# A graph network on one core: the sums start from each node's own row, and the last tiles' steps are placed anew

## The chip, the core and the metric

The kernel runs on one core of a Trainium2 chip. A core has several engines that work side by side, each with its own stream of instructions, done in order: PE multiplies matrices and transposes through a multiplication with the identity matrix; DVE does elementwise work; ACT does functions of one variable and also issues transfers; POOL (GpSimd) here does little else than gather rows of a table in memory by an index; SP issues plain transfers. An engine waits for another by semaphores. SBUF is the memory on the core, of 128 partitions; PSUM is the small memory, in banks, that PE writes its results to.

The metric is the time of one execution on the device, in microseconds (us). The kernel before takes 4307.19 us, the median of 3 runs (4305.39 to 4313.39).

## What is computed

A network over a graph of 12,500 nodes with 256 features each, and 200,000 edges sorted by their target `dst`. Cut to what matters:

```python
def gcn_conv(x, W, b, src, dst, n):          # src, dst hold the edges and one loop per node
    h = x @ W
    deg = segment_sum(ones, dst, n)
    dinv = where(deg > 0, rsqrt(deg), 0)
    return segment_sum(h[src] * (dinv[src] * dinv[dst])[:, None], dst, n) + b

h = maximum(layernorm(x), 0)
h = h @ W_pre + b_pre
h = relu(gcn_conv(h, W1, b1, src + loops, dst + loops, n))
h = relu(gcn_conv(h, W2, b2, src + loops, dst + loops, n))
x = x + h @ W_post + b_post

h = maximum(layernorm(x), 0)
xt = (h @ weight).reshape(n, 4, 64)
alpha = softmax(leaky_relu(alpha_l(xt)[src] + alpha_r(xt)[dst]), over the heads)
x = x + broadcast(sum over the heads of alpha[:n] * xt[dst[:n]])
```

Each convolution adds up, for every node, the rows of the sources of its edges and the node's own row (the loop). The last layer uses only the first n edges, one for each output row.

## The kernel before

**Tiles and chunks.** Nodes are taken 128 at a time: 98 node tiles (`NT`). Edges are taken 128 at a time too, one gather for each such group; 14 gathers (`J`) make a chunk. There are 112 chunks (`NCH`), the last one of 9 gathers, so 1563 gathers in a convolution.

**Stages.** `fast_path` first computes the degrees and the normed rows, scaled by `dinv`, and writes them to `table1` in memory. Convolution one reads `table1` and writes `table2`; convolution two reads `table2`, adds the residual and writes `table_l` and `table_r` (what the attention layer needs of each row) and `kept_x`. The attention stage gathers from those and writes the output. A table must be written in full before the first gather of the next stage reads it. For the attention stage POOL first gathers seven blocks from `table_r` (which only covers the first tiles), then, after PE and ACT have made `fxg` of the first group, gathers `fal` from `table_l` (L1199).

**The loop of a convolution** (`convolve`). The order of instructions is that of the code (`manual_schedule`). For every gather POOL brings 128 rows into one of 64 buffers `fgot` (L999). DVE has made, once per chunk, a matrix `fhot` of ones and zeros (L939) that says to which target within the chunk's window of 128 nodes each edge goes. PE multiplies the two into the PSUM bank `facc` (L1004); 14 such multiplications add up a chunk.

At the end of a chunk `close` lays out three things. ACT copies `facc` to SBUF as `fsums` (L946). Later PE transposes it into the bank `fturn` (`turn`, L952 and L954). Later still DVE adds that to a sliding buffer of sums `buf` (`add`, L962; in convolution one also a row of extra sums, L965), at a column that it reads from a register, since a chunk's window lies anywhere among the `BW` = 448 columns that the buffer covers. After an addition that completes a node tile, `shift` makes a new buffer: it zeroes the last 128 columns (L974) and copies the others down (L975; L977 and L978 for the extra row). Then the finished tile goes through the steps of `finish1` or `finish2`.

**Due times.** `close` and `shift` don't issue these steps at once. They put them into a list with a due time, counted in gathers: `at(t + 8, turn)` means after the multiplication of the eighth gather from here. `run(t)`, called after every gather's multiplication, issues what is due. The steps of a tile that need the same single PSUM bank as another tile's are held apart by `fills` and `taken`: a step that fills a bank first runs the step that reads what the bank holds.

`finish1` (offsets in gathers): 0 `a` loads the tile's own rows `self` and the row `fins` on SP; 6 `b` transposes them into the bank `fpt` (`turned`, L1014, and L1029); 8 `c` adds them to the sums into `fin` (L1033, L1034); 14 `d` multiplies by the weights into `fpo` (L1039, and L1040 for the bias); 16 `e` applies relu on ACT (L1044) and writes 128 rows of `table2` (L1045, a transfer that ACT issues).

`finish2`: 0 `a` loads own rows, `rm` and the rows `fxb` of x; 6 `b` (L1014) and 8 `c` (L1074) as above; 14 `d` first weights into `fpz` (L1080, L1082); 16 `e` relu (`fz`, L1087); 20 `f` second weights into `fpo` (L1092, L1093); 22 `g` adds the residual (`fx`, L1097), stores it to `kept_x` and takes its statistics; 24 `h` norms (L1108 to L1113); 28 `i` transposes into `fpt` (L1014); 30 `k` copies that to `ht` (L1120); 34 `q` multiplies into `fpx` (L1128); 36 `r` copies it (L1133) and writes `table_l` and, for the first tiles, `table_r` (L1134, L1136).

**The end of a convolution.** Chunk 109 completes tile 94, chunk 110 tile 95, and the last chunk the tiles 96 and 97. From chunk 109 on (`near`) the offsets are halved, and the second of the two last tiles is shifted two gathers after the first:

```python
near = c + 3 >= NCH
then = None
for o, step, fills in reversed(finish(state["w"], buf, sbuf)):
    then = at(now + (o // 2 if near else o), lambda _, step=step: step(), fills, then)
...
if state["w"] < complete[c + 1]:
    at(now + (2 if near else J), shift)
```

After the last gather `run()` issues all that is left in order of due time.

Of the kernel before, what the change touches and what calls it, by code (L numbers as in the profile page):

```python
# [17 lines left out]
P = 128  # L18
# [395 lines left out]
def fast_path(  # L414
# [58 lines left out]
    XW = (M * (AC - 1) + OFF + P - 1) // P + 1  # L473
    assert AC * J == NT and AC * CE <= E and XW <= NT
    table_r = dram.tile([XW * P, DR], F32, name="table_r")
# [412 lines left out]

    def convolve(ep, table, stride, width, ahead, with_sum, psum, finish):

# [3 lines left out]
        state = {"w": 0, "n": 0}  # L894
        due, taken = [], {}

        def at(t, step, fills=None, then=None):
# [23 lines left out]
        def new_buf():  # L921
            buf = work.tile([P, KC, BW], F32, name="buf", bufs=5)
            sbuf = work.tile([1, BW], F32, name="sbuf", bufs=5) if with_sum else None
            return buf, sbuf

        state["buf"] = new_buf()
        for b in state["buf"]:
            if b is not None:
                nc.vector.memset(b, 0.0)

# [12 lines left out]
        def close(c, acc, t):  # L943

            sb = work.tile([P, width], F32, name="fsums", bufs=3)
            nc.scalar.activation(sb, acc, AF.Copy)  # L946
            v = {}

            def turn(_):
                v["pt"] = psum.tile([P, KC + 1, P], F32, name="fturn", bufs=1)  # L950
                for k in range(KC):
                    nc.tensor.transpose(v["pt"][:, k, :], sb[:, k * P:(k + 1) * P], ident)  # L952
                if with_sum:
                    nc.tensor.transpose(v["pt"][:1, KC, :], sb[:, D:D + 1], ident)  # L954

            def add(now):
                buf, sbuf = state["buf"]
                off = nc.values_load(offs[0:1, c:c + 1], engines=(mybir.EngineType.DVE,),
                                     min_val=0, max_val=OFF,
                                     skip_runtime_bounds_check_because="clamped on the chip")  # L960
                b = buf[:, :, bass.ds(off, P)]
                nc.vector.tensor_add(b, b, v["pt"][:, :KC, :])  # L962
                if with_sum:
                    b = sbuf[:, bass.ds(off, P)]
                    nc.vector.tensor_add(b, b, v["pt"][:1, KC, :])  # L965
                shift(now)

            def shift(now):
                if state["w"] == complete[c + 1]:
                    return  # L970

                buf, sbuf = state["buf"]
                nxt, nxs = new_buf()
                nc.vector.memset(nxt[:, :, BW - P:], 0.0)  # L974
                nc.vector.tensor_copy(nxt[:, :, :BW - P], buf[:, :, P:])  # L975
                if with_sum:
                    nc.vector.memset(nxs[:, BW - P:], 0.0)  # L977
                    nc.vector.tensor_copy(nxs[:, :BW - P], sbuf[:, P:])  # L978

                near = c + 3 >= NCH  # L980
                then = None
                for o, step, fills in reversed(finish(state["w"], buf, sbuf)):
                    then = at(now + (o // 2 if near else o), lambda _, step=step: step(),
                              fills, then)
                state["w"] += 1
                state["buf"] = nxt, nxs
                if state["w"] < complete[c + 1]:
                    at(now + (2 if near else J), shift)

            at(t + 8, turn)  # L990
            at(t + 13, add)

# [17 lines left out]

    def turned(psum, s):
        pt = psum.tile([P, KC + 1, P], F32, name="fpt", bufs=1)
        for k in range(KC):
            nc.tensor.transpose(pt[:, k, :], s[:, k * P:(k + 1) * P], ident)  # L1014
        return pt


    def finish1(psum, w, buf, sbuf):
        v = {}

        def a():
            v["s"] = work.tile([P, D1], F32, name="self", bufs=4)
            nc.sync.dma_start(v["s"], table1[w * P:(w + 1) * P, :])
            v["fs"] = work.tile([2, P], F32, name="fins", bufs=4)
            nc.sync.dma_start(v["fs"][1:2, :], root_t[w:w + 1, :])

        def b():
            v["pt"] = turned(psum, v["s"])
            nc.tensor.transpose(v["pt"][:1, KC, :], v["s"][:, D:D + 1], ident)  # L1029

        def c():
            v["f"] = work.tile([P, KC, P], F32, name="fin", bufs=3)
            nc.vector.tensor_add(v["f"], buf[:, :, :P], v["pt"][:, :KC, :])  # L1033
            nc.vector.tensor_add(v["fs"][:1, :], sbuf[:, :P], v["pt"][:1, KC, :])  # L1034

        def d():
            po = v["po"] = psum.tile([P, D], F32, name="fpo", bufs=1)
            for k in range(KC):
                nc.tensor.matmul(po, v["f"][:, k, :], wf[:, k, :], start=(k == 0), stop=False)  # L1039
            nc.tensor.matmul(po, v["fs"], bb, start=False, stop=True)  # L1040

        def e():
            o = work.tile([P, D], F32, name="fo", bufs=3)
            nc.scalar.activation(o, v["po"], AF.Relu, scale=dinv2[:, w:w + 1])  # L1044
            nc.scalar.dma_start(table2[w * P:(w + 1) * P, :], o)  # L1045

        return [(0, a, None), (6, b, "fpt"), (8, c, None), (14, d, "fpo"), (16, e, None)]

    with tc.tile_pool(name="psum1", bufs=1, space=PSUM) as psum, \
            tc.tile_pool(name="edges1", bufs=1) as ep, \  # L1050
            tc.tile_pool(name="fwork1", bufs=2) as work:
        convolve(ep, table1, D1, D + 1, 64, True, psum, lambda w, b, s: finish1(psum, w, b, s))


    def finish2(psum, w, buf, sbuf):
        v = {}
        n = min(P, N - w * P)

        def a():
            v["s"] = work.tile([P, D], F32, name="self2", bufs=4)  # L1060
            nc.sync.dma_start(v["s"], table2[w * P:(w + 1) * P, :])
            v["rm"] = work.tile([1, P], F32, name="rm", bufs=4)
            nc.sync.dma_start(v["rm"], root_t[w:w + 1, :])
            v["x"] = work.tile([P, D], F32, name="fxb", bufs=4)
            if n < P:
                nc.vector.memset(v["x"], 0.0)
            nc.sync.dma_start(v["x"][:n, :], x[w * P:w * P + n, :])

        def b():
            v["pt"] = turned(psum, v["s"])  # L1070

        def c():
            v["f"] = work.tile([P, KC, P], F32, name="fin", bufs=3)
            nc.vector.tensor_add(v["f"], buf[:, :, :P], v["pt"][:, :KC, :])  # L1074

        def d():
            pz = v["pz"] = psum.tile([P, KC, P], F32, name="fpz", bufs=1)
            for m in range(KC):
                for k in range(KC):
                    nc.tensor.matmul(pz[:, m, :], wb[:, k, m * P:(m + 1) * P], v["f"][:, k, :],  # L1080
                                     start=(k == 0), stop=False)
                nc.tensor.matmul(pz[:, m, :], b2r[:, m * P:(m + 1) * P], v["rm"],  # L1082
                                 start=False, stop=True)
# [5 lines left out]
        def f():  # L1089
            po = v["po"] = psum.tile([P, D], F32, name="fpo", bufs=1)  # L1090
            for m in range(KC):
# [23 lines left out]
        def i():  # L1115
            v["pt2"] = turned(psum, v["h"])

# [7 lines left out]
        def q():  # L1125
            px = v["px"] = psum.tile([P, DA], F32, name="fpx", bufs=1)
            for k in range(KC):
                nc.tensor.matmul(px[:, d0:], v["ht"][:, k, :], wg[:, k, d0:],  # L1128
                                 start=(k == 0), stop=(k == KC - 1))

        def r():
            xa = work.tile([P, DA], F32, name="fxa")
            nc.scalar.activation(xa[:, d0:], v["px"][:, d0:], AF.Copy)  # L1133
            nc.scalar.dma_start(table_l[w * P:(w + 1) * P, :], xa[:, DR:])  # L1134
            if w < XW:
                nc.scalar.dma_start(table_r[w * P:(w + 1) * P, :], xa[:, :DR])  # L1136

        return [(0, a, None), (6, b, "fpt"), (8, c, None), (14, d, "fpz"), (16, e, None),
                (20, f, "fpo"), (22, g, None), (24, h, None), (28, i, "fpt"), (30, k, None),
                (34, q, "fpx"), (36, r, None)]  # L1140


# [15 lines left out]
    with tc.tile_pool(name="psum2", bufs=1, space=PSUM) as psum, \  # L1158
            tc.tile_pool(name="edges2", bufs=1) as ep, \
            tc.tile_pool(name="fwork2", bufs=2) as work:  # L1160
        for c in range(EARLY):
            turn_hots(ap, c, load_ends(work, c, 1), EARLY)
        convolve(ep, table2, D, D, 64, False, psum, lambda w, b, s: finish2(psum, w, b, s))

# [123 lines left out]
```

## Time and profile before

| what | us |
|---|---|
| median of 3 runs | 4307.19 |
| the profiled execution by its own clock | 4960.23 |
| its span, first to last instruction | 4958.2 |
| PE busy | 2964.7 (60%) |
| weight loads of PE (beside PE) | 2202.3 (44%) |
| POOL busy | 3115.8 (63%) |
| DVE busy | 1148.5 (23%) |
| ACT busy | 383.4 (8%) |
| gathers of both convolutions, L999, 3126 of them | 2984.3 busy, 955 ns each |

The profile is of one execution, taken with the hardware profiler; it took 653 us longer than the median of the runs. A line of the timeline gives the start, the duration (both us), the engine, the line of the kernel, the operation, what it writes and reads, and in brackets how long the engine had stood idle and what released it. The table of stretches gives for each stretch its length, the busy time of each engine with the number of its instructions, then the clock that PE was granted (1 is full speed), the share of time in which transfers ran, and the GB/s. Where it is asked for one engine alone, there is one busy column. In the table of waits a line gives an engine, what waited and what released it, and then the total wait in us, the number of waits and the longest.

### The profile page before, as it was taken

The numbers are of one execution on the slowest core, as the hardware profiler recorded it, in microseconds if no ns is written. First come the engines' busy times: TensorE is split into PE (matmuls) and PEld (weight loads), VectorE is DVE, ScalarE is ACT, GpSimd is POOL, SyncE is SP. The second block draws the span as 40 slices with busy tenths as digits, with TensorE's granted clock in tenths as the row PEclk, the third lists the DMA queues.
The fourth block names the chain that finished last, engine by engine and source line by source line (L and its number), as shares of the span: only waits on it lengthen the run. The fifth ranks groups of instructions, "written<-read, shape, count | busy, mean of one in ns | idle before, by whom it ended". The sixth has DMA issues, their size and how long they took to land.

```text
span 4958.2 us, 34772 instructions
## 1 busy us (share of the span) xinstructions
PE 2964.7 (60%) x10827; PEld 2202.3 (44%) x10827; DVE 1148.5 (23%) x2468; ACT 383.4 (8%) x1054; POOL 3115.8 (63%) x3297
## 2 busy tenths in 40 slices
PE   5345555564555556465626767666777677677853
PEld 4133444343343334344414555555555555555642
DVE  7211111121111212112202222222222222222227
ACT  3100000000000000000000000000000000000112
POOL 2566666666666666666466666666666666666533
PEclk7567777677777777777757777777777777777766
DMA  5433333333333333333333443444444443444335
GB/s 179 133 93 105 106 106 105 104 108 104 106 105 105 104 105 106 105 106 104 101 93 112 113 112 105 113 108 107 110 109 109 110 108 108 109 110 108 97 97 157
DMA packets 301046, 543.62 MB, mean 110 GB/s; under 512 B 84021, under 2 KB 199476, under 8 KB 300852
## 3 DMA queue, kind: packets, MB, share of 16 engines
q0 software_dynamic: 154480, 414.28, 31.3%
q1 hardware_dynamic: 114926, 111.19, 7.4%
q10 hardware_dynamic: 31446, 15.83, 1.1%
q8 instruction: 88, 1.44, 0.1%
q14 instruction: 106, 0.87, 0.1%
HBM read 488.01 MB, written 52.93 MB: 109 GB/s over the span
## 4 chain that ended last, share of the span: by engine, by line
another core or an unknown queue 36%; PE 32%; issue 19%; DVE 4%; ACT 3%; POOL 1%; DMA 1%; ACTq 0%; DVEq 0%; POOLq 0%; SPq 0%
PE facc L1004 18%; PE fpo L1092 3%; PE fpo L1039 2%; PE fpx L1128 2%; PE fpo L1093 2%; PE fpo L1040 1%; POOL fgot L999 1%; PE fturn L952 1%; ACT h L1113 1%; PE fpt L1014 1%; PE fpz L1080 1%; DVE fhot L939 1%; DVE fx L1097 1%; PE fpz L1082 1%
## 5 line engine op out<-in xcount | busy, mean ns | idle before, releaser
L999 POOL DMA_INDIRECT fgot<-ftable,fsrc_t x3126 | 2984.3, 955 | 1595.4 <-issue 822.5
L1004 PE MATMUL facc<-fgot,fhot 128*128 128x257 f32 (+1 forms) x6252 | 1901.8, 456 | 218.1 <-issue 157.2
L1004 PEld LDWEIGHTS facc<-fgot,fhot 128*128 128x128 f32 x6252 | 1392.8, 233 | 564.6 <-issue 297.0
L952 PE MATMUL fturn<-fident,fsums 128*128 128x128 f32 x448 | 117.3, 355 | 626.9 <-issue 484.8
L939 DVE TENSOR_TENSOR fhot<-iota_p,to_t 128x1792 f32<-128x1792 f32 x224 | 447.6, 2000 | 0.1
L952 PEld LDWEIGHTS fturn<-fident,fsums 128*128 128x128 f32 x448 | 75.9, 184 | 690.4 <-issue 529.0
L946 ACT ACTIVATE fsums<-facc 128x257 f32<-128x257 f32 (+1 forms) x224 | 86.2, 385 | 3586.5 <-remote 2411.7
L1097 DVE SCALAR_TENSOR_TENSOR fx<-fpo,fdinv,fxb 128x256 f32<-128x256 f32 x98 | 47.4, 484 | 1289.1 <-PE fpo L1093 837.2
L1039 PE MATMUL fpo<-wf,fin 128*128 128x256 f32 x392 | 142.4, 499 | 329.1 <-issue 242.9
L1128 PE MATMUL fpx<-fwg,ht 128*128 128x4 f32 (+1 forms) x392 | 99.1, 363 | 391.3 <-ACT ht L1120 359.5
L1033 DVE TENSOR_TENSOR fin<-buf,fpt 128x256 f32<-128x256 f32 x98 | 41.1, 420 | 1205.5 <-remote 916.9
L962 DVE TENSOR_TENSOR buf<-buf,fturn 128x256 f32 x224 | 94.5, 422 | 949.8 <-PE facc L1004 414.4
L1128 PEld LDWEIGHTS fpx<-fwg,ht 128*128 128x128 f32 x392 | 88.6, 300 | 427.4 <-ACT ht L1120 388.7
L1039 PEld LDWEIGHTS fpo<-wf,fin 128*128 128x128 f32 x392 | 93.8, 252 | 362.0 <-issue 330.3
L1092 PE MATMUL fpo<-fwo,fz 128*128 128x256 f32 x392 | 171.8, 584 | 80.7 <-ACT fz L1087 78.8
L1199 POOL DMA_INDIRECT fal<-table_l,fsrc_t x98 | 94.0, 959 | 140.4 <-ACT fxg L1192 84.6
L1080 PE MATMUL fpz<-fin,fwb 128*128 128x128 f32 x784 | 147.5, 317 | 10.3 <-issue 10.3
L1092 PEld LDWEIGHTS fpo<-fwo,fz 128*128 128x128 f32 x392 | 104.7, 291 | 102.2 <-ACT fz L1087 83.4
L1080 PEld LDWEIGHTS fpz<-fin,fwb 128*128 128x128 f32 x784 | 118.3, 215 | 26.6 <-issue 16.3
L1190 PE MATMUL fends<-rows,hot_t 128*128 128x260 f32 x196 | 71.2, 517 | 86.8 <-issue 48.4
L1014 PE MATMUL fpt<-fident,self 128*128 128x128 f32 x392 | 100.6, 343 | 22.4 <-issue 19.6
L1014 PE MATMUL fpt<-fident,h 128*128 128x128 f32 x196 | 42.7, 303 | 108.6 <-ACT h L1113 83.0
(176 smaller groups left out, 1754.9 us busy)
## 6 DMA issues: line engine op xcount, KB each, us to landing
fgot<-ftable,fsrc_t POOLq DMA_INDIRECT x3126
ftable<-fxt SPq DMA_DIRECT2D x14, 910.0 KB
self<-ftable SPq DMA_DIRECT2D x98, 130.0 KB
ftable<-fo ACTq DMA_DIRECT2D x98, 128.0 KB
self<-ftable SPq DMA_DIRECT2D x98, 128.0 KB
kept_x<-fx SPq DMA_DIRECT2D x98, 128.0 KB
fxr<-kept_x SPq DMA_DIRECT2D x14, 896.0 KB
fxb<-in_x_dram SPq DMA_DIRECT2D x97, 128.0 KB
```

The costliest lines, as they stand in the source:

```text
L939: nc.vector.tensor_tensor(h[:, :n, :], iota_p[:, None, :].to_broadcast([P, n, P]), to_t[:, c, :n, None].to_broadcast([P, n, P]), ALU.is_equal)
L952: nc.tensor.transpose(v["pt"][:, k, :], sb[:, k * P:(k + 1) * P], ident)
L962: nc.vector.tensor_add(b, b, v["pt"][:, :KC, :])
L999: nc.gpsimd.indirect_dma_start(out=got, out_offset=None, in_=table[:], in_offset=bass.IndirectOffsetOnAxis(ap=src_t[:, c, j:j + 1], axis=0))
L1004: nc.tensor.matmul(acc, hots[c][:, j, :], got[:, :width], start=(j == 0), stop=(j == nj[c] - 1))
L1014: nc.tensor.transpose(pt[:, k, :], s[:, k * P:(k + 1) * P], ident)
L1039: nc.tensor.matmul(po, v["f"][:, k, :], wf[:, k, :], start=(k == 0), stop=False)
L1080: nc.tensor.matmul(pz[:, m, :], wb[:, k, m * P:(m + 1) * P], v["f"][:, k, :], start=(k == 0), stop=False)
L1092: nc.tensor.matmul(po, v["z"][:, m, :], wo[:, m, :], start=(m == 0), stop=False)
L1093: nc.tensor.matmul(po, v["rm"], bor, start=False, stop=True)
L1097: nc.vector.scalar_tensor_tensor(x2, v["po"], dinv[:, w:w + 1], v["x"], op0=ALU.mult, op1=ALU.add)
L1128: nc.tensor.matmul(px[:, d0:], v["ht"][:, k, :], wg[:, k, d0:], start=(k == 0), stop=(k == KC - 1))
```

## The change

The change has three parts, all in `convolve` and what it calls.

First, a node's own row is no longer added at the end, by steps `a` to `c` of its tile, but begins the sums. At the start of a convolution `load_rows` brings the rows of the first 448 nodes, PE transposes them into `fturn`, and DVE copies them into `buf`. Later, when a chunk completes a tile, the rows of the 128 nodes that come into the buffer's last columns are transposed beside the chunk's sums, into the second half of `fturn`, and a copy from PSUM takes the place of the zeroing. These rows, and what the tile's steps read (`prepare`), are loaded when the tile before is shifted (`ready`).

Second, the weights' multiplications read the first 128 columns of `buf` in place; `fin`, and for the own rows `fpt`, are gone. The tile's steps are then fewer and their offsets shorter: 6 and 10 in `finish1`, 6 to 28 in `finish2`.

Third, the end: from chunk 109 on, the transposition comes 4 and the addition 6 gathers after the chunk (1 and 2 for the last chunk), the steps of a tile follow one gather apart, a second shift follows at once, and the very last tile's steps write to PSUM banks of their own (`in_psum`): a bank of `facc`, `fturn` or `iota_p`, which are free by then. Before, both last tiles shared one bank of each name.

```diff
-    def convolve(ep, table, stride, width, ahead, with_sum, psum, finish):
+    def convolve(ep, table, stride, width, ahead, with_sum, psum, prepare, finish):
...
+        new_rows = [max(min(P, NT * P - P * w - BW), 0) for w in range(NT)]
...
+        def load_rows(n0, n):
+            s = work.tile([P, stride], F32, name="self", bufs=4)
+            if n < P:
+                nc.vector.memset(s, 0.0)
+            nc.sync.dma_start(s[:n, :], table[n0:n0 + n, :])
+            return s
+
+        def turn_sums(rows, i, v):
+            for k in range(KC):
+                nc.tensor.transpose(v["pt"][:, i * KC + k, :], rows[:, k * P:(k + 1) * P], ident)
+            if with_sum:
+                nc.tensor.transpose(v["ps"][:, i, :], rows[:, D:D + 1], ident)
+
+        def new_turned(v):
+            v["pt"] = psum.tile([P, 2 * KC, P], F32, name="fturn", bufs=1)
+            if with_sum:
+                v["ps"] = psum.tile([1, 2, P], F32, name="fsum", bufs=1)
+
         state["buf"] = new_buf()
-        for b in state["buf"]:
-            if b is not None:
-                nc.vector.memset(b, 0.0)
+        for n0 in range(0, BW, P):
+            v, n = {}, min(P, BW - n0)
+            new_turned(v)
+            turn_sums(load_rows(n0, n), 0, v)
+            nc.vector.tensor_copy(state["buf"][0][:, :, n0:n0 + n], v["pt"][:, :KC, :n])
+            if with_sum:
+                nc.vector.tensor_copy(state["buf"][1][:, n0:n0 + n], v["ps"][:, 0, :n])
+
+        def ready(w):
+            if w < NT:
+                n = new_rows[w]
+                state["next"] = prepare(w), load_rows(P * w + BW, n) if n else None
+
+        ready(0)
...
             def turn(_):
-                v["pt"] = psum.tile([P, KC + 1, P], F32, name="fturn", bufs=1)
...
+                new_turned(v)
+                turn_sums(sb, 0, v)
+                if complete[c + 1] > state["w"] and state["next"][1] is not None:
+                    turn_sums(state["next"][1], 1, v)
...
             def shift(now):
-                if state["w"] == complete[c + 1]:
+                w = state["w"]
+                if w == complete[c + 1]:
                     return
 
                 buf, sbuf = state["buf"]
-                nxt, nxs = new_buf()
-                nc.vector.memset(nxt[:, :, BW - P:], 0.0)
-                nc.vector.tensor_copy(nxt[:, :, :BW - P], buf[:, :, P:])
...
+                pre, rows = state["next"]
+                steps = finish(w, buf, sbuf, pre)
+                if w + 1 < NT:
+                    nxt, nxs = new_buf()
+                    nc.vector.tensor_copy(nxt[:, :, :BW - P], buf[:, :, P:])
+                    if rows is None:
+                        nc.vector.memset(nxt[:, :, BW - P:], 0.0)
+                    else:
+                        nc.vector.tensor_copy(nxt[:, :, BW - P:], v["pt"][:, KC:, :])
...
-                for o, step, fills in reversed(finish(state["w"], buf, sbuf)):
-                    then = at(now + (o // 2 if near else o), lambda _, step=step: step(),
-                              fills, then)
+                for i, (o, step, fills) in reversed(list(enumerate(steps))):
+                    then = at(now + (i + 1 if near else o), lambda _, step=step: step(), fills, then)
                 state["w"] += 1
-                state["buf"] = nxt, nxs
+                ready(w + 1)
                 if state["w"] < complete[c + 1]:
-                    at(now + (2 if near else J), shift)
-
-            at(t + 8, turn)
-            at(t + 13, add)
+                    shift(now)
+
+            at(t + (1 if c + 1 == NCH else 4 if near else 8), turn)
+            at(t + (2 if c + 1 == NCH else 6 if near else 13), add)
...
+    def in_psum(psum, w, name, shape, other, other_shape, bufs=1):
+        if w + 1 < NT:
+            return psum.tile(shape, F32, name=name, bufs=1)
+        return psum.tile(other_shape, F32, name=other, bufs=bufs)
+
+    def fills(w, name):
+        return name if w + 1 < NT else name + "_last"
...
-            po = v["po"] = psum.tile([P, D], F32, name="fpo", bufs=1)
+            po = v["po"] = in_psum(psum, w, "fpo", [P, D], "facc", [P, D + 1], 3)[:, :D]
             for k in range(KC):
-                nc.tensor.matmul(po, v["f"][:, k, :], wf[:, k, :], start=(k == 0), stop=False)
-            nc.tensor.matmul(po, v["fs"], bb, start=False, stop=True)
+                nc.tensor.matmul(po, buf[:, k, :P], wf[:, k, :], start=(k == 0), stop=False)
+            nc.tensor.matmul(po, fs, bb, start=False, stop=True)
...
-        return [(0, a, None), (6, b, "fpt"), (8, c, None), (14, d, "fpo"), (16, e, None)]
+        return [(6, d, fills(w, "fpo")), (10, e, None)]
...
-        return [(0, a, None), (6, b, "fpt"), (8, c, None), (14, d, "fpz"), (16, e, None),
-                (20, f, "fpo"), (22, g, None), (24, h, None), (28, i, "fpt"), (30, k, None),
-                (34, q, "fpx"), (36, r, None)]
+        return [(6, d, fills(w, "fpz")), (8, e, None), (12, f, fills(w, "fpo")), (14, g, None),
+                (16, h, None), (20, i, fills(w, "fpt")), (22, k, None),
+                (26, q, fills(w, "fpx")), (28, r, None)]
```

## The prediction

> **What bounds the kernel now.** I cut the profiled execution where its stages end, by the stretches of busy time: the work ahead of the first gather, convolution one, the turn to convolution two, convolution two, the turn to the attention stage, the attention stage.
>
> ```profile
> core 0: us, PE busy (x) PEld busy (x) DVE busy (x) ACT busy (x) POOL busy (x), PEclk, DMA share, GB/s
> 162.00:2393.30 2231.30, 1184.30 (x4179) 867.80 (x4180) 417.48 (x875) 74.29 (x198) 1493.09 (x1563) 0.71 0.38 104
> 2393.30:2437.60 44.30, 38.62 (x167) 28.33 (x165) 17.77 (x51) 4.91 (x12) 0.02 (x1) 0.87 0.11 33
> 2437.60:4678.10 2240.50, 1516.03 (x5574) 1141.63 (x5575) 475.10 (x945) 188.97 (x558) 1491.18 (x1563) 0.74 0.41 110
> 4678.10:4771.40 93.30, 83.12 (x332) 62.15 (x332) 25.46 (x69) 15.85 (x47) 6.62 (x7) 0.74 0.15 40
> 4771.40:4958.20 186.80, 68.02 (x190) 43.64 (x189) 104.65 (x186) 38.31 (x112) 93.95 (x98) 0.63 0.52 159
> ```
>
> With the 162.0 us ahead these make the span, 4958.2; the execution took 4960.2, so 2 us lie around it. The timeline of POOL shows the cuts: gathers start 1.25 us apart (0.95 for the instruction, 0.30 between two) until the last of a convolution, and then POOL stands still until what it reads next is written.
>
> ```profile
> 2391.12 0.95 POOL L999 DMA_INDIRECT fgot<-ftable,fsrc_t  x1 [0.30 <-issue]
> 2392.37 0.95 POOL L999 DMA_INDIRECT fgot<-ftable,fsrc_t  x1 [0.30 <-issue]
> ...
> 2437.60 0.94 POOL L999 DMA_INDIRECT fgot<-ftable,fsrc_t  x1 [44.29 <-issue]
> ...
> 4677.14 0.94 POOL L999 DMA_INDIRECT fgot<-ftable,fsrc_t  x1 [0.30 <-issue]
> ...
> 4771.43 0.94 POOL L1199 DMA_INDIRECT fal<-table_l,fsrc_t  x1 [84.59 <-ACT fxg L1192]
> ```
>
> Each convolution issues 1563 gathers: 1563 x 1.25 = 1953.8 us. The two stages took 277.5 and 286.7 more. POOL's own busy time is 1493.1 and 1491.2 where 1563 x 0.945 is 1477.0, so 30.3 of these 564 are gathers that lasted longer; the other 534 are waits in which several engines start again together, and whose end the table of waits can't name (for POOL: `POOL fgot L999 <- remote: 483.1, 277, 11.0`).
>
> The median of the runs shown is 4307.2, 653 under this execution. Take the 534 away. Through those waits TensorE ran behind POOL by its 64 buffers, and each turn also holds the work it had left; without it a turn is a landing, one multiplication and the chain behind it (below): 18.2 in place of 44.3, and 47.3 in place of 93.3. That is 606 of the 653. So I read the timed runs as: the gathers' pace of 1.25 us throughout, nearly 91% of the time, and two exposed chains. A change is worth what it does to the pace and to these chains; I subtract it from 4307.2.
>
> **The chain at each turn**, from the end of the last multiplication of a gather to POOL's next start, by the timeline:
>
> ```profile
> 2421.26 0.60 PE L1004 MATMUL facc<-fgot,fhot 128*128 128x257 f32 x2
> ...
> 2434.61 0.33 ACTq L1045 DMA_DIRECT2D ftable<-fo  x1
> ...
> 4726.06 0.60 PE L1004 MATMUL facc<-fgot,fhot 128*128 128x256 f32 x2
> ...
> 4767.80 0.33 ACTq L1134 DMA_DIRECT2D table_l<-fxa  x1
> ```
>
> First turn: 2421.86 to 2437.60 is 15.7 us, 3.0 of it the landing of the last write. Second: 4726.66 to 4771.43 is 44.8, 3.6 of it landing. Ahead of it stand the landing of the last gather (3.0 taken, less its 0.95 of issue) and a multiplication of 0.43: 18.2 and 47.3.
>
> **First turn, changed.** Now chunk 110 is added after the last gather, and tiles 95, 96 and 97 follow with the own row's transposes and one bank `fpo`. After the change tile 95 is done before the last gather is multiplied (its chunk is added 6 gathers after it closed), and behind the last gather there are: eviction 0.44, three transposes 0.54 to 0.85, add 0.47, six matmul records of tile 96 and six of 97 with no wait between them (each tile 1.76 warm, 3.23 in the last rows of the stage), ACT and issue 0.55, landing 3.0. Sum 8.5 (warm) to 11.8. Saved 4 to 7; I take **5**.
>
> **Second turn, changed.** Removed behind the last gather: the second half of tile 94, the first half of 95, all the own-row transposes and adds, and the waits for one `fpz`, `fpo`, `fpt`, `fpx`. What remains, warm/cold: `fpo` of 95 1.65/3.22; its chain over DVE and ACT to `h` 2.56; transposes 0.44/0.69; `fpz` of 96 and 97 2 x 2.07/2 x 3.8; `fpx` of 95 0.5/1.0; `fpo` of both 2 x 1.65/2 x 3.22; norm of both 3.1 (2.56, and a second `h` of 0.6 on ACT); transposes, copy, `fpx`, copy, issue 1.6/2.3; landing 3.6. With hand-overs of 0.1: 20.9 warm, 30.6 cold. The row that decides which:
>
> ```profile
> 4720.00:4730.00 10.00, 8.51 (x43) 1.00 0.09 26
> 4730.00:4740.00 10.00, 8.03 (x29) 0.51 0.19 53
> ...
> 4722.87 0.61 PE L1080 MATMUL fpz<-fin,fwb 128*128 128x128 f32 x4
> 4734.65 1.20 PE L1080 MATMUL fpz<-fin,fwb 128*128 128x128 f32 x4
> ```
>
> The granted clock fell to 0.5 four us into the chain, and stayed there for 41 us though PE was busy 0.7 to 0.9 of it. [...] by the row it stays cold. I go by the row, with a few warm us at the start: 27. Saved 14 to 24; **18**.
>
> **The pace.** At each of the 196 shifts the copy of the sums (L975) and the zeroing ahead of it (L974) can hold a gather:
>
> ```profile
> 3519.14 0.27 DVE L974 MEMSET buf<- 128x256 f32 x1
> 3519.33 1.24 POOL L999 DMA_INDIRECT fgot<-ftable,fsrc_t  x1 [0.30 <-PE facc L1004]
> 3519.33 0.43 DVE L975 COPY buf<-buf 128x640 f32<-128x640 f32 x1
> ```
>
> The 30.3 us above are these: 0.15 a shift. The zeroing goes (0.70 us unbroken becomes 0.43) and a copy from PSUM takes its place. If the hold goes with the length of the pair, 0.39 x 29 = **11** are saved. [...] I stay with 11. Bounds: 29 saved, or a loss (last rival): no row shows a copy from PSUM beside a gather.
>
> **Costed at nothing.** (1) The rows that begin the sums: four loads, eight or twelve transposes, four copies and a zeroing per convolution stand on SP, PE and DVE ahead of `iota_p`, the first `fhot` and the first multiplication, which comes some 6 us later (in the second convolution SP also has three `to_all` ahead, 13 us of issue). POOL does not wait for it: 64 buffers cover 80 us, of which 20.6 are used now (2437.60 to 2458.25). Without the cover: 6 us each. (2) In every tile the own row's transposes move into the chunk's turn, beside its sums; the load is issued a tile ahead, so over 17 us before, against 3 of landing. Were it late, PE would stand in order with the gathers' multiplications behind it, and POOL 64 gathers later. (3) Dropped additions (0.42, and 0.27 in the first) and the copy that replaces the zeroing: DVE is busy a fifth of these stages. (4) SP's count of loads and stores per tile is the same; `kept_x` waits for DVE in it as before.
>
> **Sum.** 5 + 18 + 11 = 34: 4307 - 34 = **4273 us**. Against its own execution the same 34, with the waits on top, which I can't forecast.
>
> **Rivals.** *Late before the last gather*: from chunk 109 on a tile's steps stand one gather apart (1.25 us), but `fpo` to `h` takes 2.56 and cold `fpz` 3.8. PE waits in order, the gathers' multiplications behind it, and reaches the last one 5 to 13 us late: gain 34 - 18 = 16, 4291. For it: the granted clock; against: ten or more gathers of slack between the tiles. *Held at every shift*: in an even pace each shift may meet POOL at the same moment. Now 0.36 as in the longest rows of convolution two, 70 us; then 0.1, 20: 50 + 23 saved, 4234. *The turn is set by something else*: `fal` also waits for the new pools' space. Then only the first turn counts, 4302, no change to be measured. Against: what ACT waited for at 4770.76 was the landing of `table_l`. *Slower*: the new copies from PSUM (0.42) hold GpSimd like L975. Unbroken 0.85 us; a gather that meets its start is held 0.72, at 196 shifts 141 for 30 now: 4307 + 111 - 23 = 4395. It decides from a mean hold of 0.27 us a shift, where 30 + 23 are used up. Against: their duration. L653, a copy from PSUM, needs 414 ns for 256 elements, L975 428 for 640[...].
>
> **How the numbers follow.** Chances: as summed 0.60 (by itself 4252 to 4290), late 0.15, held at every shift 0.08, something else 0.09, slower 0.08. 0.2%, 8.6 us, is about what a measurement of this kernel tells from no change. Faster by more: 0.59 + 0.13 + 0.08 + 0.02 = 0.82; within 0.10; slower 0.08. The range 4245 to 4302 leaves out 0.08 below and some 0.11 above.
>
> **What would show it.** In the changed profile: from the last `facc` of a gather to the next POOL start about 11 and 27 us; no row on `fpt<-fident,self`; POOL's busy time in the two stages nearer 1477 each, and no gather over 1.0 us beside a copy from PSUM alone. Wrong would be: starts of gathers further apart than 1.25 with no wait between, the first gather after 162 us, or a `fturn` that waits for `self`.

## The result, and the profile after

The changed kernel takes 4282.2 us (median of 4 runs, 4280.3 to 4282.8) where the kernel before took 4306.3 beside it: a ratio of 0.995, with a 95% interval of 0.9938 to 0.9962. By the medians that is 24.1 us saved, by the ratio 21.5 (16 to 27), where 34 were forecast. The time lies inside the range; the likeliest case named a gain of the right kind, from three sources, and one of the three gave nothing.

On some of the chips every kernel took 4953 to 5008 us, with hundreds of waits for semaphores that arrived late (so in the profile of the kernel before, and not in that of the changed kernel), and each time is therefore set against the kernel before on the same chip.

The stretches of busy time of the changed kernel, cut at the same places, without the work ahead of the first gather (the two turns, the second and the fourth row, here begin at the end of the last gather of a convolution and end with the first gather from the next table):

```profile
core 0: us, PE busy (x) PEld busy (x) DVE busy (x) ACT busy (x) POOL busy (x), PEclk, DMA share, GB/s
161.80:2128.77 1966.97, 1577.99 (x4318) 859.64 (x4317) 419.38 (x823) 88.04 (x206) 1491.06 (x1563) 0.76 0.44 119
2128.77:2140.37 11.60, 7.28 (x27) 4.19 (x25) 1.93 (x8) 1.81 (x4) 0.00 (x0) 0.94 0.16 49
2140.37:4108.11 1967.74, 1557.45 (x5817) 1037.71 (x5818) 476.75 (x900) 212.12 (x585) 1491.79 (x1563) 0.85 0.48 126
4108.11:4138.20 30.09, 25.80 (x91) 18.39 (x90) 5.59 (x19) 6.37 (x19) 6.87 (x7) 0.63 0.20 52
4138.20:4279.90 141.70, 65.31 (x192) 49.19 (x190) 105.56 (x186) 38.16 (x112) 94.86 (x98) 0.72 0.69 210
```

Both convolutions now run at the gathers' pace from end to end: 1563 x 1.25 is 1953.8, and the two stages take 1967.0 and 1967.7. The 534 us of waits that the profile before showed are not there, as the reading of the timed runs supposed: in the table of waits POOL's longest wait for PE is 0.3 us, and its one wait of 11.6 is the first turn.

```profile
POOL fgot L1043 <- issue: 474.2, 1519, 11.6
POOL fgot L1043 <- PE facc L1048: 382.3, 1255, 0.3
```

POOL's busy time, though, is 1491 and 1492 in the two stages, as before (1493 and 1491). Over both convolutions the gathers last longer than 945 ns each by 28.8 us in sum, where it was 30.2; this sum is called the excess below.

The timeline at the two turns: the last multiplications of gathers, the last write of a table, POOL's first gather from that table.

```profile
2130.92 1.13 PE L1048 MATMUL facc<-fgot,fhot 128*128 128x257 f32 x4
...
2137.47 0.33 ACTq L1083 DMA_DIRECT2D ftable<-fo  x1
...
2140.37 0.94 POOL L1043 DMA_INDIRECT fgot<-ftable,fsrc_t  x1 [11.60 <-issue]
...
4110.46 1.13 PE L1048 MATMUL facc<-fgot,fhot 128*128 128x256 f32 x4
...
4135.82 0.33 ACTq L1169 DMA_DIRECT2D table_l<-fxa  x1
...
4138.20 0.94 POOL L1235 DMA_INDIRECT fal<-table_l,fsrc_t  x1 [21.09 <-ACT fxg L1228]
```

From 2132.05 (2130.92 + 1.13) to 2140.37 the first chain takes 8.3 us, for 15.7 before; from 4111.59 to 4138.20 the second takes 26.6, for 44.8. The clock did in the second turn what it did before:

```profile
4110.00:4120.00 10.00, 8.10 (x36) 6.14 (x35) 2.88 (x9) 2.49 (x7) 5.59 (x6) 0.80 0.45 115
4120.00:4130.00 10.00, 10.00 (x28) 6.49 (x26) 1.09 (x3) 0.85 (x3) 0.00 (x0) 0.50 0.05 13
4130.00:4140.00 10.00, 7.61 (x23) 5.66 (x23) 1.62 (x7) 3.87 (x11) 1.50 (x2) 0.50 0.20 51
```

PE is busy for all of the second of these stretches, and the granted clock (the third number from the end) stays at 0.5.

### The profile page after: what moved, and what is told of

Same layout as the page of the kernel before. It is cut to its first block, busy times and chain, and to the rows that moved or that the text cites. A ratio compares the mean times of both kernels' runs of the same rounds, so it can differ in the third digit from the quotient of the medians.

```text
span 4279.9 us, 35030 instructions
## 1 busy us (share of the span) xinstructions
PE 3309.1 (77%) x10832; PEld 2027.9 (47%) x10832; DVE 1116.9 (26%) x2279; ACT 407.6 (10%) x1054; POOL 3115.8 (73%) x3297
## 5 line engine op out<-in xcount | busy, mean ns | idle before, releaser
L1048 PE MATMUL facc<-fgot,fhot 128*128 128x257 f32 (+1 forms) x6252 | 2385.5, 500 | 774.3 <-DMA fgot<-ftable,fsrc_t 738.5
L1048 PEld LDWEIGHTS facc<-fgot,fhot 128*128 128x128 f32 x6252 | 1233.1, 230 | 1784.6 <-DMA fgot<-ftable,fsrc_t 1451.2
L1077 PE MATMUL fpo<-wf,buf 128*128 128x256 f32 x388 | 162.3, 565 | 0.4 <-DVE buf L997 0.4
L1112 PE MATMUL fpz<-buf,fwb 128*128 128x128 f32 x776 | 147.2, 319 | 0.0
L1077 PEld LDWEIGHTS fpo<-wf,buf 128*128 128x128 f32 x388 | 118.3, 305 | 30.8 <-DVE buf L997 0.7
L1112 PEld LDWEIGHTS fpz<-buf,fwb 128*128 128x128 f32 x776 | 121.2, 220 | 14.9 <-issue 3.6
L941 PE MATMUL fturn<-fident,self 128*128 128x128 f32 x396 | 89.5, 314 | 34.7 <-DMA self<-ftable 30.0
L1114 PE MATMUL fpz<-rm,fb2r 1*128 1x128 f32 x388 | 104.3, 352 | 0.0
L1013 DVE COPY buf<-buf 128x640 f32<-128x640 f32 x194 | 97.5, 502 | 3.3
L1078 PE MATMUL fpo<-bb,fins 2*128 2x256 f32 x194 | 87.3, 537 | 0.0
```

Of the source, the lines that this page charges most:

```text
L941: nc.tensor.transpose(v["pt"][:, i * KC + k, :], rows[:, k * P:(k + 1) * P], ident)
L1048: nc.tensor.matmul(acc, hots[c][:, j, :], got[:, :width], start=(j == 0), stop=(j == nj[c] - 1))
L1077: nc.tensor.matmul(po, buf[:, k, :P], wf[:, k, :], start=(k == 0), stop=False)
L1078: nc.tensor.matmul(po, fs, bb, start=False, stop=True)
L1112: nc.tensor.matmul(pz[:, m, :], wb[:, k, m * P:(m + 1) * P], buf[:, k, :P], start=(k == 0), stop=False)
```

## The experiments

What was to be told apart: are the 24 us the two turns (theory), or did the holds at the shifts give a part of them and the turns less (rival)? And why did the holds stay?

### The kernel before once more

No edit.

> The kernel before, unchanged, profiled once more; the profiled execution shown so far held 534 us of waits that the one of the changed kernel doesn't hold. Theory (the turns gave all of it): from the end of the last gather to POOL's next start 18 and 47 us, as read out of the disturbed execution, against 11.6 and 30.1 now; together 24 us, and the gathers lasted longer than 0.945 us by 29 to 31 us in sum, as after (28.8). Rival (the pace gave 11 of it): in an even pace the gathers of the kernel before lose some 40 us in sum, and the two turns are about 13 us longer than now together, 55 in all.

Measured: 4962.7 us, beside 4967.5 for the same kernel. The semaphores were late, so the turns' whole length says nothing; but the chains behind the last multiplication do: 12.6 and 44.1 us, for 15.7 and 44.8 in the first profile. Excess of the gathers: 33.3 us. The first chain, in the first profile and in this one, by the stretches of PE:

```profile
2421.86:2437.60 15.74, 10.05 (x30) 0.64 0.10 31
...
2430.06:2442.62 12.56, 6.87 (x30) 0.90 0.13 39
```

The same 30 instructions keep PE busy for 10.05 us at a granted clock of 0.64, and for 6.87 at 0.90.

The same kernel twice more:

> The kernel before, unchanged, for a profile without the late semaphores. Theory (the two turns gave all 24 us of the change, the holds none): from the end of the last gather to POOL's next start 18 us in the first turn and 47 us in the second, against 11.6 and 30.1 in the changed kernel, and the gathers' excess over 0.945 us stands within 3 us of the changed kernel's 28.8. Rival (the holds gave a part): the excess is 35 to 45 us and the turns are shorter by as much.

> The kernel before, unchanged, for its own profile without late semaphores. Theory (the change is worth its two turns): from the end of the last gather to POOL's next start 15 to 18 us in the first turn (12.6 to 15.7 behind the last multiplication in the disturbed profiles, and some 3 before it) and 47 us in the second, together 21 to 24 us over the changed kernel's 41.7; the gathers' excess over 0.945 us within 3 us of the 28.1 of the kernel with the new end alone, whose long stages are the same. If the turns are shorter than that by more than 5 us, something else than they holds part of the 24 us. If the semaphores are late again: nothing new.

They gave 4993 and 4998.5 us, the semaphores late both times, with chains of 15.8 and 44.1, and 12.6 and 44.3, and an excess of 32.9 and 34.1. The first chain has two values 3.2 apart: 12.6 in the two profiles where the clock in it was 0.90 and 0.98, and 15.7 to 15.8 where it was 0.64 and 0.63. So the chains can be read with late semaphores too, but only to some 3 us: the second repeats within 0.7 us here, and is 30.7, 30.8 and 33.6 in three profiles of the kernel with the new end alone, below. No profile shows a whole turn of the kernel before without late semaphores; it is put together from its chain and the 3.0 to 3.5 us that the last gather's landing and multiplication take in the changed kernel and in that with the own rows alone: 15.6 to 19.2, and 47.1 to 48.3.

### The own rows alone

To the changed kernel, the old end (so the first two parts of the change without the third):

```diff
...
-                    then = at(now + (i + 1 if near else o), lambda _, step=step: step(), fills, then)
+                    then = at(now + (o // 2 if near else o), lambda _, step=step: step(), fills, then)
...
-                    shift(now)
+                    at(now + (2 if near else J), shift)
...
-            at(t + (1 if c + 1 == NCH else 4 if near else 8), turn)
-            at(t + (2 if c + 1 == NCH else 6 if near else 13), add)
+            at(t + 8, turn)
+            at(t + 13, add)
...
-        if w + 1 < NT:
-            return psum.tile(shape, F32, name=name, bufs=1)
-        return psum.tile(other_shape, F32, name=other, bufs=bufs)
+        return psum.tile(shape, F32, name=name, bufs=1)
...
```

> The changed kernel with the old end: due times 8 and 13 for every chunk, halved offsets in the last tiles, the second shift two gathers later, one PSUM bank of each name. Theory (turns alone): the pace is that of the kernel before, the own row's transposes and additions leave the chains, worth some 3 us in the first turn and 6 in the second: 4297 us. Rival (the pace gave 11): 4286 us. If the old end alone set the turns: 4306 us.

> Once more the changed kernel with the old end. In the first attempt, where all kernels stood at 4966 us, the chains from the last multiplication to POOL's next start were 10.2 and 32.9 us (kernel before 12.6 to 15.7 and 44.1 to 44.8, changed kernel 8.3 and 26.6), and the gathers' excess was 12.0 us. Theory (turns alone, excess as before): 4306 less 2 to 5 less 11.5, 4291 us. If the smaller excess of that run is the edit's own doing and not the phase of that execution: 4274 us.

> The changed kernel with the old end, a third time, for its time on a chip without late semaphores. Its chains were 10.2 and 32.9 to 34.3 us in the first two attempts (changed kernel 8.3 and 26.6). Where the kernel before takes some 4305 us: theory (time follows the two chains, and the gathers' excess is that of the changed kernel, 28.8 us, since the long stages are the same code) 8 to 10 us more than the changed kernel's ratio gives, 4290 us; rival (the new end lengthened the excess, and the old one leaves it at some 11 us as in the two disturbed runs) 4274 us. Where the kernel before takes 4960 us or more: the same within 0.2%.

The first two ran beside a kernel before of 4967 and 4995 us (ratios 1.0003 and 0.9992, both intervals with 1 inside): they told the chains, not the time. The third, 4300.3 us beside 4310.8, gives 0.9975 (0.9965 to 0.9985), 10.4 us saved by the medians. Its turns, by the timeline of POOL:

```profile
2146.42 0.95 POOL L1043 DMA_INDIRECT fgot<-ftable,fsrc_t  x1 [12.97 <-issue]
...
4151.99 0.94 POOL L1233 DMA_INDIRECT fal<-table_l,fsrc_t  x1 [27.77 <-ACT fxg L1226]
```

12.97 in the first turn, and in the second 36.55 (its last gather ended at 4115.44). Chains of 10.0 and 33.5: the own rows alone are worth some 3 to 6 us in the first turn and 11 in the second. The excess was 33.8 us, so the small ones of the disturbed profiles (12.0 and 9.9) belonged to those executions and not to the edit. In this execution the 2201 gathers that no DVE instruction crossed took 948 ns each in place of 946 in the changed kernel, which is 4 of the 5 us by which its excess is larger. The turns would give 13 to 18 us; the interval of the time runs from 6.5 to 15.1, so no shortfall is shown.

### The new end alone

To the kernel before, the new due times and the banks of the last tile; own rows are still added at the end of each tile:

```diff
...
-                    then = at(now + (o // 2 if near else o), lambda _, step=step: step(),
-                              fills, then)
+                    then = at(now + (i + 1 if near else o), lambda _, step=step: step(), fills, then)
...
-            at(t + 8, turn)
-            at(t + 13, add)
+            at(t + (1 if c + 1 == NCH else 4 if near else 8), turn)
+            at(t + (2 if c + 1 == NCH else 6 if near else 13), add)
...
-        pt = psum.tile([P, KC + 1, P], F32, name="fpt", bufs=1)
+        pt = in_psum(psum, w, "fpt", [P, KC + 1, P], "fturn", [P, KC + 1, P])
...
```

> The kernel before with the new end alone: due times 4 and 6 (1 and 2 for the last chunk), steps one gather apart, second shift at once, the last tile in banks of its own; own rows are still added at the end of each tile, and the zeroing stays. Theory (turns alone): some 5 us less in the first turn, 12 in the second: 4289 us. Rival (the pace gave 11 of 24): the end brings 13 less what the own rows' steps cost, 4297 us.

> Once more the kernel before with the new end alone. In the first attempt its chains were 14.0 and 30.7 us. Theory (turns alone): 4306 less 0 to 2 less 13.7, 4291 us. Sum of this and of the run before it: 30 us saved against 24 for the whole change, as both take the own rows' steps of the last tiles off the same chain or pack them.

> The kernel before with the new end alone, a third time, for its time without late semaphores, and because its long stages are those of the kernel before, zeroing included. Chains in the two disturbed runs: 14.0 to 15.2 and 30.7 us. Theory (the change is worth its two chains, the zeroing holds nothing): the gathers' excess is 28 to 34 us, as in the changed kernel; from the last gather to POOL's next start 17 and 34 us; 0.3% faster than the kernel before, some 4292 us where that takes 4306. Rival (the long stages of the kernel before lose more to holds in an even pace than the changed kernel's 28.8 us): an excess of 40 us or more. Where the kernel before takes 4960 us or more: the same within 0.2%.

Again the first two (1.0 and 1.0003) told the chains alone. The third: 4298.7 us beside 4302.9, a ratio of 0.9986 (0.9978 to 0.9995); by the medians 4.2 us saved, by the ratio 6.0, where 14 were expected. Turns of 19.3 us (nothing saved at a like clock: its chain is 15.9 at a granted clock of 0.61, for 15.7 at 0.64 before) and of 40.0, by the timeline of POOL:

```profile
2149.88 0.94 POOL L998 DMA_INDIRECT fgot<-ftable,fsrc_t  x1 [19.28 <-issue]
...
4114.23 1.34 POOL L998 DMA_INDIRECT fgot<-ftable,fsrc_t  x1 [0.30 <-issue]
...
4155.59 0.95 POOL L1208 DMA_INDIRECT fal<-table_l,fsrc_t  x1 [31.25 <-ACT fxg L1201]
```

Packed as they are, the own rows' steps now stand in PE's way:

```profile
4118.15 0.70 PE L1003 MATMUL facc<-fgot,fhot 128*128 128x256 f32 x2 [1.03 <-DMA fgot<-ftable,fsrc_t]
4121.14 0.41 PE L1021 MATMUL fpt<-fident,self 128*128 128x128 f32 x2 [2.29 <-DMA self<-ftable]
4121.38 0.60 PE L1003 MATMUL facc<-fgot,fhot 128*128 128x256 f32 x2
```

A tile's own row is loaded when the tile is shifted and transposed one gather later. PE waits 2.29 us for it, and the last gather's multiplication stands behind (6.4 us after the gather's end; 3.5 in the changed kernel). The 2.9 us more are those of the late row; the changed kernel loads it a tile ahead.

Whether the two parts are worth more together than apart the times don't settle: by the medians 10.4 + 4.2 is 14.6 where both gave 24.1, by the ratios 10.8 + 6.0 is 16.8 where both gave 21.5, and each interval reaches some 4 to 5 us to either side. By the profiles the two turns together are 59.3 us with the new end alone, 49.5 with the own rows alone and 41.7 with both, for 62.7 to 67.5 before: the sum of the parts lies within some 4 us of the whole.

This run settles the rival too. Its long stages are those of the kernel before, zeroing included, and in an even pace: an excess of 28.1 us, for 28.8 in the changed kernel. Counting only the gathers that lasted more than 20 ns too long, it is 26.0 us here, 25.4 in the changed kernel and 24.0 with the own rows alone: each is one execution, and they agree within 2 us. The holds gave nothing that can be told from zero.

### The copies of the sums on ACT

```diff
-                    nc.vector.tensor_copy(nxt[:, :, :BW - P], buf[:, :, P:])
+                    nc.scalar.activation(nxt[:, :, :BW - P], buf[:, :, P:], AF.Copy)
...
-                        nc.vector.tensor_copy(nxs[:, :BW - P], sbuf[:, P:])
+                        nc.scalar.activation(nxs[:, :BW - P], sbuf[:, P:], AF.Copy)
```

> The changed kernel, with the copies from the old sliding buffer to the new one on ACT in place of DVE; the copies from PSUM stay on DVE. Theory (the SBUF to SBUF copy on DVE holds the gathers, the copy from PSUM does not): the sum by which gathers last longer than 0.945 us falls from 28.8 to about 2, and the time by the same, to 4255 us. Rival (the copy from PSUM holds them too): at least half of the 28.8 stays, 4268 us or more. If holds are made good elsewhere: 4282 us with the holds gone.

> The same edit once more (the copies from the old sliding buffer to the new one on ACT, those from PSUM on DVE), since in the four runs before this one every kernel, that of before too, stood at 4966 us with hundreds of waits for late semaphores, and nothing that shortens POOL's chain could show. Where the kernel before takes some 4306 us: theory (the SBUF to SBUF copy on DVE holds the gathers, the copy from PSUM does not) 4255 us, the gathers' excess down from 28.8 to about 2; rival (the copy from PSUM holds too) 4268 us or more with at least half of the excess left; if the holds are made good elsewhere, 4282 us with the excess gone. Where the kernel before takes some 4966 us again: 4966 us, and nothing is told apart.

Both met late semaphores: 4965.5 us beside 4967.5 (0.9997, interval 0.9988 to 1.0006) and 4988.0 beside 4996.1 (0.9977, 0.9965 to 0.999). The holds were gone all the same: the excess was 2.4 and 2.2 us. The copies from PSUM, left on DVE, hold gathers for no more than that.

### The zeroing put back, without the copies

To the edit above:

```diff
+                        nc.vector.memset(nxt[:, :, BW - P:], 0.0)
                         nc.vector.tensor_copy(nxt[:, :, BW - P:], v["pt"][:, KC:, :])
```

> As the run before this (copies between the sliding buffers on ACT), and on DVE the zeroing of the new columns put back ahead of the copy from PSUM that fills them. It measures the zeroing's own hold on the gathers, from which the prediction took its 11 us. If the zeroing holds gathers as the copy does: the sum by which the gathers last longer than 0.945 us, 2.2 us in the run before, rises by 5 to 15 us. If only the copy with two sides in SBUF holds them: it stays below 4 us. Time: where the kernel before takes some 4306 us, 4255 us if the zeroing holds nothing and removed holds are time saved, 4282 us if removed holds are made good elsewhere; where it takes some 4970 to 5000 us, the same within 0.3% and nothing told by the time.

4260.7 us (4256.8 to 4262.3) beside 4303.5: a ratio of 0.9897 (0.988 to 0.9913), the fastest kernel of the study, 43 us under the kernel before and half a per cent under the change. The excess is 3.1 us. In the timelines of POOL and DVE, first the changed kernel, where the copy (L1013) starts with a gather:

```profile
1338.38 1.30 POOL L1043 DMA_INDIRECT fgot<-ftable,fsrc_t  x1 [0.30 <-DMA fgot<-ftable,fsrc_t]
1338.39 0.47 DVE L1013 COPY buf<-buf 128x640 f32<-128x640 f32 x1
1338.79 0.41 DVE L1017 COPY buf<-fturn 128x256 f32<-128x256 f32 x1
```

and here, where the zeroing (L1017) and the copy from PSUM (L1018) stand inside one:

```profile
1141.06 0.94 POOL L1044 DMA_INDIRECT fgot<-ftable,fsrc_t  x1 [0.30 <-issue]
1141.08 0.27 DVE L1017 MEMSET buf<- 128x256 f32 x1
1141.39 0.42 DVE L1018 COPY buf<-fturn 128x256 f32<-128x256 f32 x1
```

1.30 us against 0.94. In this run 263 gathers are crossed by a zeroing or a copy from PSUM, and all of them together last 0.1 us too long. In the changed kernel 103 gathers met the copy from SBUF to SBUF of L1013 and were held by more than 30 ns, 23.7 us in sum.

The span against the changed kernel's: 4260.5 for 4279.9, 19.4 less. Removed holds 28.8 - 3.1 = 25.7; the turns were 16.9 and 31.1 us for 11.6 and 30.1, 6.3 more; the difference is 19.4. That the 5.3 us more in the first turn come from the clock and not from the edit is likely, but not shown: with the copies on ACT and no zeroing the first chain was 8.4 in both runs above, where the clock in it was 0.86 and 0.96, and it is 11.6 here:

```profile
2115.84:2132.74 16.90, 12.62 (x27) 6.63 (x26) 1.45 (x6) 2.90 (x6) 0.00 (x0) 0.51 0.11 32
```

The granted clock of this first turn is 0.51, and 0.94 in the changed kernel's. As in the kernel before, the chain of the first turn is some 3 us longer at the lower clock.

## Why the prediction was right, and where it failed

**What bounds the kernel.** Right, and it carried the rest: the gathers' pace and two exposed chains. The waits of the profile shown were rightly taken away before anything was summed; that the timed runs don't hold them is shown by the profile after. It also shows most of the 47 us that the prediction's reading left over (606 of 653): the attention stage took 186.8 us in the profile before and takes 141.7 now, and 141.8 with the new end alone, where that stage is unchanged.

**The first turn: 5 us, from a chain of 8.5 warm to 11.8 cold.** The chain was 8.3 warm (granted clock 0.96 in it), and 11.6 cold (0.50) in the run with the zeroing put back. At roughly like clocks the gain is the same, 4.2 us: 12.56 - 8.31 warm, 15.74 - 11.56 cold. Against the warm 8.3 it is 4.3 to 7.4, by the clock that the kernel before met; that part is luck and not the change. Right within its range.

**The second turn: 18 us, a chain of 27.** 26.6, for 44.1 to 44.8: 17.5 to 18.2 saved. What the granted clock would do decided it. With the clock up all through the sum was 20.9, an estimate for a turn that no profile shows; with the clock at 0.5, as in the row of the kernel before, it was 30.6; 27 was taken, with a guess at how long the clock would stay up. It fell to 0.5 at 4116.1, 4.5 us into the chain, and was 0.50 for the 22.1 us that were left of it, through more than 10 us of an entirely busy PE: the row held.

**The pace: 11 us. This step failed.** "If the hold goes with the length of the pair" was the assumption: a zeroing of 0.27 us ahead of the copy was taken to hold gathers as the copy does, so that dropping it would shorten the hold by 0.39 of itself. The 0.70 us of the pair were misread as well: in the row that the prediction shows the two overlap, and from the zeroing's start to the copy's end it is 0.62. The zeroing alone holds nothing (0.1 us in 263 crossings, above). What holds is the copy from SBUF to SBUF (103 gathers, 23.7 us, above), and that copy stayed: on 194 shifts in place of 196, and at 502 ns each in place of 433. Only where the copy follows did a zeroing stand in a hold: in the first profile six gathers, all in convolution one, were held to the copy's end though at their first moment (0.12 us in; see the last section) only the zeroing ran.

```profile
401.02 1.45 POOL L999 DMA_INDIRECT fgot<-ftable,fsrc_t  x1 [0.30 <-issue]
401.04 0.27 DVE L974 MEMSET buf<- 128x256 f32 x1
401.24 0.42 DVE L975 COPY buf<-buf 128x640 f32<-128x640 f32 x1
```

These six are 3.1 us, and five such in the kernel with the new end alone 2.6. They are gone with the zeroing, and the sum did not fall: the excess is 28.1 us with the kernel before's long stages and 28.8 with the changed ones, so the term was 11 and measured -0.7, which is the 10 us between 34 and 24. Why other holds took the place of those six no run shows.

**Costed at nothing.** Right. The first multiplication came 4.1 us later in the first convolution (8.0 for 3.9 to 4.0 after the first gather) and 6.2 in the second (26.8 for 20.6), the 6 that were named, and POOL's first gather started at 161.8 us, as before (162.0). The load one tile ahead cost nothing either; the new end alone, where the row is loaded late, lost 2.9 us in the way that the prediction had named.

**The rivals.** *Late before the last gather* was priced at 18 us and happened as 0.3 to 0.4: PE finished the last gather 3.3 and 3.5 us after POOL in the changed kernel, 3.0 and 3.1 with the old end. It came true where it had not been looked for, in the new end without the own rows (3 us). *Held at every shift*: no; 103 gathers were held at 194 shifts. Its premise, that removed holds are time saved one for one, was right: 25.7 us of them were worth 25.7. *The turn is set by something else*: no; `fal` started 2.4 us after the last write of `table_l` was issued. *Slower, the copies from PSUM hold GpSimd*: no; in the run with the zeroing put back the crossings of both, 263, cost 0.1 us.

Against the sum as measured: 4.3 to 7.4, 17.5 to 18.2, and -0.7, less 0.7 for reaching the last gathers later, give 20 to 24 (20 to 21 with the first turn at like clocks); the runs say 24.1 by the medians and 21.5 by the ratio. That the total came out right owes much to a wide range: any gain from 5 to 62 us lay inside it, so a term of 11 could be missing. The two turns are what the prediction had right by its own reasons.

## What to carry to other kernels

Where a stage runs at one engine's pace, cost a change by what it does to that pace and to the exposed ends, and give each term to the one instruction that earns it: of three DVE instructions at a shift (zeroing, copy, copy from PSUM), the copy held the gathers, and it was the one that the change kept. Ask of each DVE instruction near a gather on GpSimd whether it copies from SBUF to SBUF, and look at the gathers that it crosses; with this copy on ACT and the zeroing put back the span was 19.4 us shorter still, nearly as much again as the whole change. And before a tail is packed, what it reads has to be loaded earlier: otherwise PE stands for it with the last gathers behind (2.29 us with the new end alone).

## What the runs showed of the hardware

In the changed kernel the copy of the sums holds a gather only if it covers one of two moments, some 0.12 us and some 0.82 us after the gather's start; it then lasts until the copy's end and its remaining time. In the row above the copy ends 0.48 us into the gather: 0.48 - 0.12 = 0.36 more than 0.945 is the 1.30 seen. A copy that lies from 0.28 to 0.75 us into a gather adds 2 ns. It can also be the copy that is held: 28 of the 194 copies started 0.52 to 0.78 us into a gather that kept its 0.94 to 0.96 us, and lasted 0.54 to 0.74 us themselves, where the median is 0.49.

Not every copy from SBUF to SBUF holds. That of one row of 128 elements (`fins<-sbuf`) stayed on DVE in the three runs with the other copies on ACT; it covered the first moment 28 times there, and none of those gathers lasted more than 2 ns over 945. In every profile three gathers at the start of convolution two, 0.9 to 2.3 us of the excess in sum, are held under another DVE instruction from SBUF to SBUF, the TENSOR_SCALAR that makes `hot_t` from `to_all`.

On the chips where every kernel took some 4960 to 5000 us, PE's increments of its semaphore reached the other engines late and in bundles. Their recorded times are less than 60 ns apart some 1190 to 1360 times in each of the ten such executions profiled, and never in the four others. In the first run with the copies on ACT, by its timeline:

```profile
586.13 0.63 PE L941 MATMUL fturn<-fident,self 128*128 128x128 f32 x2
586.56 0.42 PE L943 MATMUL fsum<-fident,self 128*1 128x128 f32 x1
...
600.98 0.42 DVE L997 TENSOR_TENSOR buf<-buf,fturn 128x256 f32 x1 [18.86 <-issue]
...
601.55 2.05 PE L1077 MATMUL fpo<-wf,buf 128*128 128x256 f32 x4 [9.71 <-issue]
...
603.30 0.94 POOL L1043 DMA_INDIRECT fgot<-ftable,fsrc_t  x1 [3.54 <-remote]
```

PE's transposes were done at 587; DVE's addition, whose other inputs had long been written, starts 14 us later, PE stands 9.7 us for DVE's sum, and POOL 3.5 for a buffer. There POOL isn't the bound: each part of the change alone, and the whole of it with the holds removed, were worth nothing or next to it (ratios 0.9977 to 1.0003). What delays the increments no run shows.
